# A two-layer graph network: weight rows loaded over two queues, an earlier norm, and layer 1's products split into y and v columns

## Chip, cores and metric

One NeuronCore of a Trainium2 chip runs the whole program. The metric is the device time of one execution in microseconds; the number for the kernel before is the median of three runs.

## What is computed

There are 128 graphs (B) of 128 nodes (N) with 512 features (D), all in float32. Every graph passes through two layers, each behind a layer norm with ReLU, and each adding its result to x. Cut to what matters:

```python
# layer 0
h = maximum(layernorm(x), 0)
Xw = h @ Wv + bv
e = leaky_relu((Xw @ aw[:d])[:, None, :] + (Xw @ aw[d:])[:, :, None] + ab, 0.2)
T = adj * exp(e);  T = T / (T.sum(-1) + 1e-12)
x = x + relu(h @ Wk[0] + bk[0] + (T @ h) @ Wk[1] + bk[1] + (T @ T @ h) @ Wk[2] + bk[2])
# layer 1
h = maximum(layernorm(x), 0)
q, k = split(h @ Wqk);  v = h @ Wv1
w = mask * sum(q * (adj @ (k * mask)), -1) / sqrt(512)
x = x + softmax(w over the nodes)[:, None] * v
```

## The kernel before, in words

The graphs are taken in 64 pairs (`G = 2`, `NP = 64`). Weights are folded first. The columns of Wv times the two halves of aw become two extra columns beside Wk[2] (`r2`, W2). Wk[1] and Wk[0] stand side by side in `r10` (W1). The product of Wq and Wk of layer 1 is formed once (`score_matrix`, L240) as 512 columns, called y's, in `rl[:, :, 0]`; Wv1 is put beside it in `rl[:, :, 1]`. So layer 1 needs only y = h · M and v = h · Wv1, and the score of a node is y times its row of adj · h.

All large products go through `strassen` (L322): the left side is split into two graphs by two halves of the 512 inner features, the right side into two inner halves by two column halves, and seven block products (numbers 1 to 7) stand in for eight. The sums that this needs are formed by VectorE: `left_sums` (L310) per pair, `combine` (L160) once per weight set, four instructions each. Four PSUM banks a, b, c, e collect the blocks; ScalarE copies hand partial results from bank to bank between products (L340 to L348).

Per pair p, the main loop (L625 and on) has TensorE do: `y10(p)` (h · Wk[1] and h · Wk[0] in banks a1, b1, c1, e1), `inner` and `outer` (the two products with T), `y2(p + 1)` for the next pair in banks a2, b2, c2, e2, then `layer1(p - 1)` in the same four banks. `attention` (L390) forms T on VectorE and ScalarE. `norm0` and `norm2` make h; `by_blocks` (L285) sends h to DRAM on SP's queue (`hd`) and reads it back in blocks (`hv`), so that VectorE can transpose it in 32x32 blocks (L299). The first pair and layer 1 of the last pair are transposed on TensorE instead.

In layer 1 before the change, the two column halves of the Strassen split each hold half of y and half of v: block (j, nh) is, for graph j, y[:, half nh] and v[:, half nh]. A score therefore needs both blocks of its graph. For the last pair, `layer1` forms the adj · h products early and scores graph 0 at the sixth product and graph 1 in two half scores (L500), the second of them after the seventh product; `finish_graph` (L529) spreads a score over the partitions by a transpose on TensorE and forms the softmax factor (`weights`, L556), and `result` (L574) adds factor times v to x1 and stores it.

The order on each engine is made by a scheduler from program order and data dependences; `issue_after` and `behind` (L70) add edges that keep an instruction behind a named one on the same engine. Every engine works its instructions off in order. A tile pool's buffers and at most eight outstanding DMAs per kind of queue hold a DMA issue back until an earlier one has landed.

The start is as follows. SP's queue issues x of pair 0 (L121), Wqk in eight pieces (L122 to L125), Wv (`rows(wv0_sb, ...)`, L150), Wk[2] (L151), x of pair 1 (L152) and Wk[1], Wk[0] (L154). `rows` (L144) loads a 512x512 weight in four DMAs, each of which fills 32 partitions (chunk c fills partitions 32c to 32c + 31, from 128 rows of the weight). GpSimd's queue loads small vectors and adj in blocks (`agb`, L93). TensorE runs dummy products (`warm`, L182; four at the start, six more behind the attention vectors, L594), transposes Wqk (`weights_transposed`, L225; ScalarE copies the banks out), transposes h of pair 0, forms the score matrix, then `y2(0)` and `y10(0)`. VectorE forms the attention columns (L199), the sums for r2, then those for r10 (L609) and then attention(0) and pair 1's norm (L618).

Of the kernel before, what the change touches and what calls it, by code (L numbers as in the profile page):

```python
# [15 lines left out]
def kernel(  # L16
# [64 lines left out]
    def load_x(p):  # L81
        xg[p] = loads.tile([P, G, D], FP, name="xg")
        nc.sync.dma_start(xg[p], x[p * G:(p + 1) * G].rearrange("b n d -> n b d"))
# [38 lines left out]
    for c in range(DC):  # L122
        for a in range(2):
            at = slice(a * D, (a + 1) * D)
            nc.sync.dma_start(wqk_sb[:, c, at], wqk[c * P:(c + 1) * P, at])  # L125
# [16 lines left out]
    nc.gpsimd.memset(bias_e[:, 0], 0.0)  # L142

    def rows(dst, w):  # L144

        for c in range(DC):
            nc.sync.dma_start(dst[c * S32:(c + 1) * S32],
                              w[c * P:(c + 1) * P].rearrange("(f a) o -> a f o", a=S32))

    rows(wv0_sb, wv0)  # L150
    rows(r2[:, :, 1:1 + D], wk[2])  # L151
    load_x(1)  # L152
    for k in range(2):
        rows(r10[:, :, k], wk[1 - k])  # L154

    def spread(dst, col):

        nc.tensor.transpose(dst, col.to_broadcast([P, P]), ident)
# [66 lines left out]
    def weights_transposed():  # L225

        banks = [a2, e2, a1, b1, c1, e1]
        for c in range(DC):
            for a in range(2):
                bank = banks[(c * 2 + a) % len(banks)]  # L230
                pt = bank.rearrange("p (o i) -> p o i", o=DC)
                for o in range(DC):
                    at = a * D + o * P
                    nc.tensor.transpose(pt[:, o, :], wqk_sb[:, c, at:at + P], ident)
                if a:
                    nc.scalar.copy(wkt[:, :, c * P:(c + 1) * P], pt)
                else:
                    nc.scalar.copy(wqt[:, :, :, c, :], pt.rearrange("p o (f a) -> p o f a", f=Q))
# [41 lines left out]
    wcols = [const.tile([P, S32], FP, name=f"wcol{i}") for i in range(3)]  # L280
    for t in wcols:
        nc.gpsimd.memset(t, 0.0)
# [190 lines left out]
    def layer1(p, steps={}):  # L473

        if p + 1 < NP:
            yv = late["p"].tile([P, G, 2, 2, HD], FP, name="yv")
        else:
            yv = t10[:, :2].rearrange("p t c o -> p (t c o)").rearrange(
                "p (j h k d) -> p j h k d", j=G, h=2, k=2)
        o = {(j, nh): yv[:, j, nh].rearrange("p k d -> p (k d)") for j in range(G) for nh in range(2)}  # L480
        s = late["p"].tile([P, 2, D], FP, name="s1")
        w = wcols[p % 3]
        last = p == NP - 1

        def end12(b, t):
            nc.vector.tensor_add(o[0, 1], b, t)
            if last:
                score(p, yv, w, a1, 0)
                late["w"] = finish_graph(p, yv, w, 0, b1)
            else:  # L490
                aggregate(p, 0, a2)

        def end22(e, t):
            nc.vector.tensor_add(o[1, 1], e, t)
            if last:
                half_score(e1[:, HD:], yv[:, 1, 1, 0, :], 3)

        def half_score(y, agg, at):
            junk = front.tile([P, D], FP, name="junk", bufs=1)
            nc.vector.scalar_tensor_tensor(junk[:, :HD], y, wscale[:, B - 1:B], agg, op0=OP.mult,  # L500
                                           op1=OP.mult, accum_out=w[:, at:at + 1])

        def end21(c):
            if last:
                half_score(c[:, :HD], agg, 1)
                nc.vector.tensor_add(w[:, 1:2], w[:, 1:2], w[:, 3:4])
            nc.scalar.copy(o[1, 0], c)
            if last:
                factors = finish_graph(p, yv, w, 1, c1)
                behind("peak", result, p, yv, late["w"], slice(0, 1))  # L510
                result(p, yv, factors, slice(1, 2))

        if last:
            agg = front.tile([P, G, 2, HD], FP, name="zz", bufs=1)[:, 0, 0]
            steps = {1: lambda: (aggregate(p, 0, a1), aggregate(p, 1, e1),
                                 nc.scalar.copy(agg, e1[:, :HD]), end(small.tile([P, G], FP, name="peak")))}

        strassen(set2, LEFT2.pop(p), rightl, s, True, {
            (0, 0): lambda a: nc.scalar.copy(o[0, 0], a),
            (1, 1): end22,  # L520
            (0, 1): end12,
            (1, 0): end21}, steps)
        if not last:
            aggregate(p, 1, e2)
            score(p, yv, w, a2, 0)
            score(p, yv, w, e2, 1)
        return yv, w, s

    def finish_graph(p, yv, w, j, bank):  # L529

        pw = bank[:, :G * N].rearrange("p (g n) -> p g n", g=G)
        spread(pw[:, j, :], w[:, j:j + 1])
        return weights(small.tile([P, G], FP, name="peak"), w, pw, slice(j, j + 1))

    def score(p, yv, w, agg, j):

        junk = front.tile([P, D], FP, name="junk", bufs=1)
        b = p * G + j
        nc.vector.scalar_tensor_tensor(
            junk.rearrange("p (k d) -> p k d", k=2), agg.rearrange("p (k d) -> p k d", k=2),  # L540
            wscale[:, b:b + 1], yv[:, j, :, 0, :], op0=OP.mult, op1=OP.mult,
            accum_out=w[:, j:j + 1])
# [31 lines left out]
    def result(p, yv, factors, graphs=slice(0, G)):  # L574
        x1 = X1[p]
        for at, j in enumerate(range(G)[graphs]):
            o = x1[:, j, :].rearrange("p (k d) -> p k d", k=2)
            nc.vector.scalar_tensor_tensor(o, yv[:, j, :, 1, :], factors[:, at:at + 1], o,
                                           op0=OP.mult, op1=OP.add)
        nc.sync.dma_start(out[p * G:(p + 1) * G][graphs].rearrange("b n d -> n b d"), x1[:, graphs])  # L580
# [13 lines left out]
    behind("vector", warm, 6)  # L594
    with tc.issue_after(done["warm"]):
        weights_transposed()
# [7 lines left out]
    with tc.issue_after(done["u"]):  # L604
        right2 = combine(halves(r2, W2), [t2[:, i] for i in range(4)])
    for f in range(Q):
        score_matrix(f)
    with tc.issue_after(done["right"]):
        right10 = combine(halves(r10, HD), pairs(t10))  # L609
    with tc.issue_after(done["right"]), tc.issue_after(done["m"]):  # L610
# [3 lines left out]
        for p in range(2):  # L614
            load_adj(p)
        spread_columns(0)
        attention(0, front.tile([P, D], FP, name="junk", bufs=1)[:, :G * N])
        norm0(1)  # L618
# [6 lines left out]
    for p in range(NP + 1):  # L625
# [38 lines left out]
        if p > 0:  # L664
            def last_left():
# [4 lines left out]
            yv, w, s = layer1(p - 1, {2: lambda: behind("u2", norm2), 3: last_left if p == NP - 1 else lambda: None}  # L670
                              if p < NP else {})
            if p < NP:
                ends.append((p - 1, yv, w, spread_scores(w)))
# [4 lines left out]
        if p == 0:  # L678
            rightl = behind("t", combine, halves(rl, HD), pairs(tl))
# [27 lines left out]
```

## Time and profile before

| What | Value |
|---|---|
| three runs, median | 2324.96 us (2322.57 to 2326.97) |
| profiled execution, its time | 2326.3 us |
| profiled execution, span from first to last instruction | 2324.5 us |
| granted TensorE clock, mean | 0.999 |
| one pair in the middle, 1000 to 1036 us | TensorE busy 36.00 of 36.00 us, VectorE 21.46, ScalarE 16.31, GpSimd 5.33 |
| first score product / y2(0) / y10(0) on TensorE | from 18.27 / 32.11 / 40.95 us |
| layer 1 of the last pair on TensorE | from 2302.22 us |
| last result on VectorE | 2320.29 to 2321.04 us |

In the profile PE is TensorE's matmul, PEld its weight load, DVE is VectorE, ACT is ScalarE, POOL is GpSimd, SP the engine that issues most DMAs; SPq is its queue. L12 is line 12 of the kernel. A float32 product appears as two records, so a 128-row, 512-column product takes about 0.86 us in two passes. A group line has the engine, the line, the operation, the tile written and the tiles read, a count and, in brackets, the idle time before it with what ended it. "A <- B: 1.7, 1, 1.7" in a list of waits says that A stood idle until B, 1.7 us in all, once, at longest 1.7 us. Releasers are inferred from semaphores.

### The profile page before, as it was taken

How to read it: one execution, taken by the hardware profiler on the slowest of the kernel's cores; microseconds unless marked ns; L12 is line 12 of the kernel's file. 1: busy time of each engine (PE TensorE's matmuls, PEld its weight loads, DVE VectorE, ACT ScalarE, POOL GpSimd, SP SyncE). 2: the span in 40 equal slices, each digit the busy share in tenths (PEclk: the TensorE clock that was granted, in tenths of full speed). 3: DMA queues.
4: the chain of work that ended last, by engine and by line, in shares of the span. 5: the costliest groups of instructions: out<-in, count | busy, mean ns of one | idle time of the engine just before them, and what ended most of it. 6: DMA issues, size and time to landing. Idle time of an engine off the chain costs nothing.

```text
span 2324.5 us, 23775 instructions
## 1 busy us (share of the span) xinstructions
PE 2307.6 (99%) x6901; PEld 1292.3 (56%) x6901; DVE 1362.3 (59%) x4134; ACT 1029.2 (44%) x2518; POOL 336.6 (14%) x585
## 2 busy tenths in 40 slices
PE   9999999999999999999999999999999999999998
PEld 5555555555555555555555555555555555555554
DVE  4655656556566566565565665665665656656654
ACT  4444444444444444444444444444444444444443
POOL 2011111111111111111111111111111111111100
PEclk9999999999999999999999999999999999999999
DMA  7533333333333333333333333333333333333311
GB/s 158 138 105 101 110 104 97 115 96 99 114 95 109 106 101 109 104 98 114 98 97 116 93 109 109 100 108 103 98 114 98 97 118 91 109 111 98 105 62 50
DMA packets 248133, 241.56 MB, mean 104 GB/s; under 512 B 25870, under 2 KB 171278, under 8 KB 248002
## 3 DMA queue, kind: packets, MB, share of 16 engines
q1 hardware_dynamic: 227632, 215.01, 29.5%
q0 software_dynamic: 20368, 25.03, 5.0%
q8 instruction: 54, 0.88, 0.2%
q14 instruction: 77, 0.63, 0.1%
q10 hardware_dynamic: 2, 0.00, 0.0%
HBM read 140.20 MB, written 99.74 MB: 103 GB/s over the span
## 4 chain that ended last, share of the span: by engine, by line
PE 96%; DMA 2%; DVE 1%; ACT 0%; issue 0%; SPq 0%; POOL 0%; DVEq 0%; ACTq 0%; POOLq 0%
PE c L333 23%; PE b L333 23%; PE a L333 23%; PE e L333 12%; PE e L471 2%; PE a L471 2%; PE b L459 1%; PE a L449 1%; PE c L449 1%; PE c L459 1%; PE a L459 1%; PE b L449 1%; PE e L459 1%; PE e L449 1%; PE a L420 1%; DMA r<-in_L_gnn_Wk_dram 1%
## 5 line engine op out<-in xcount | busy, mean ns | idle before, releaser
L333 PE MATMUL a<-r,x 128*128 128x257 f32 (+1 forms) x1024 | 373.3, 486 | 4.7 <-DMA ag<-in_adj_dram 1.7
L93 POOL DMA_DIRECT2D agb<-in_adj_dram x256 | 152.2, 599 | 834.0 <-DVE t L406 777.3
L371 DVE TENSOR_TENSOR y<-e,s 128x257 f32<-128x257 f32 x64 | 27.3, 427 | 406.6 <-ACT s L348 406.6
L333 PEld LDWEIGHTS a<-r,x 128*128 128x128 f32 x1024 | 189.1, 190 | 110.7 <-issue 93.2
L333 PE MATMUL a<-rl,x 128*128 128x512 f32 x512 | 240.7, 592 | 0.3 <-PE c L333 0.3
L348 ACT COPY s<-c 128x512 f32<-128x512 f32 (+1 forms) x192 | 97.9, 510 | 209.3 <-PE c L333 209.3
L333 PE MATMUL c<-t,sx 128*128 128x257 f32 (+1 forms) x512 | 186.5, 486 | 1.2 <-ACT c L344 1.2
L333 PE MATMUL b<-t,sx 128*128 128x257 f32 (+1 forms) x512 | 186.5, 487 | 0.2 <-ACT b L340 0.2
L333 PE MATMUL b<-r,sx 128*128 128x257 f32 (+1 forms) x512 | 186.5, 486 | 0.0
L333 PE MATMUL e<-t,sx 128*128 128x257 f32 (+1 forms) x512 | 186.4, 486 | 0.0
L333 PE MATMUL c<-t,x 128*128 128x257 f32 (+1 forms) x512 | 186.4, 486 | 0.0
L379 POOL DMA_DIRECT2D pzd<-pzt x62 | 36.9, 595 | 961.5 <-DVE pzt L377 916.1
L344 ACT COPY c<-b 128x512 f32<-128x512 f32 (+1 forms) x192 | 95.8, 499 | 179.1 <-PE b L333 177.6
L342 ACT COPY s<-e 128x512 f32<-128x512 f32 (+1 forms) x192 | 99.0, 515 | 157.8 <-PE e L333 157.8
L299 DVE STREAM_TRANSPOSE x<-hv 128x512 f32<-128x512 f32 x252 | 163.6, 687 | 8.8 <-DMA hv<-hd 8.7
L333 PEld LDWEIGHTS a<-rl,x 128*128 128x128 f32 x512 | 97.2, 190 | 95.8 <-issue 91.8
L340 ACT COPY b<-a 128x512 f32<-128x512 f32 (+1 forms) x192 | 96.1, 501 | 99.5 <-PE a L333 91.8
L333 PEld LDWEIGHTS c<-t,sx 128*128 128x128 f32 x512 | 96.9, 190 | 70.1 <-issue 60.0
L262 DVE TENSOR_TENSOR r<-r 128x2 f32<-128x2 f32 x128 | 20.0, 156 | 197.1 <-ACT r L261 196.9
L333 PEld LDWEIGHTS b<-t,sx 128*128 128x128 f32 x512 | 97.0, 190 | 69.2 <-issue 46.6
L333 PEld LDWEIGHTS c<-t,x 128*128 128x128 f32 x512 | 96.9, 190 | 69.3 <-issue 60.7
L333 PEld LDWEIGHTS b<-r,sx 128*128 128x128 f32 x512 | 97.1, 190 | 68.2 <-issue 61.2
(214 smaller groups left out, 3919.0 us busy)
## 6 DMA issues: line engine op xcount, KB each, us to landing
hd<-h SPq DMA_DIRECT2D x126, 512.0 KB, 2.8
hv<-hd SPq DMA_DIRECT2D x504, 128.0 KB, 2.6
xg<-in_x_dram SPq DMA_DIRECT2D x64, 512.0 KB, 3.8
out_dram<-x SPq DMA_DIRECT2D x63, 512.0 KB, 4.2
agb<-in_adj_dram POOLq DMA_DIRECT2D x256, 32.0 KB, 2.0
ag<-in_adj_dram SPq DMA_DIRECT2D x64, 128.0 KB, 2.5
pw<-pwd POOLq DMA_DIRECT2D x63, 128.0 KB, 3.3
pz<-pzd POOLq DMA_DIRECT2D x62, 128.0 KB, 3.6
```

What stands on the lines that cost most here:

```text
L93: nc.gpsimd.dma_start(agb[p][c * S32:(c + 1) * S32].rearrange("p g q i -> p (g q) i"), v[c])
L299: nc.vector.transpose(dst[:, j].rearrange("p f (n b) -> p f n b", n=Q), hv[:, j].rearrange("p n (f a) -> p f n a", f=Q))
L333: done["product"] = nc.tensor.matmul(bank, left[i][:, k * P:(k + 1) * P], right[i][:, k], start=(start and k == 0), stop=(k == HC - 1), sk ...
L340: nc.scalar.copy(b, a)
L342: nc.scalar.copy(s[:, 0], e)
L344: done["u2"] = nc.scalar.copy(c, b).ins
L348: nc.scalar.copy(s[:, 1], c)
L371: (1, 1): lambda e, t: nc.vector.tensor_add(y[:, 1, 1], e, t),
L379: nc.gpsimd.dma_start(d.rearrange("g q b -> q g b"), t[::S32])
L449: nc.tensor.matmul(bank[:, :HD], TT[p][:, j, :], y[:, j, nh, 1 - nh:W2 - nh], start=False, stop=True, skip_group_check=True)
L459: nc.tensor.matmul(bank[:, HD:], tt[:, j, :], z[:, j, nh], start=False, stop=True, skip_group_check=True)
L471: nc.tensor.matmul(to, AT[p][:, j, :], h2, start=True, stop=True)
```

## The change

It has three parts.

*Start.* Wqk is loaded in four DMAs instead of eight. A one-column copy on GpSimd, the gate, reads a column of Wqk's second quarter; behind it on GpSimd's queue are issued x of pair 1 and the upper two chunks (partitions 64 to 127) of Wv, Wk[2], Wk[1] and Wk[0]. The lower two chunks stay on SP's queue. The six dummy products ahead of the weight transposes go, and the transposes stand directly behind the attention vectors. Two of the four Wkt copies go from ScalarE to VectorE. The adj loads of pairs 0 and 1 are written ahead of the score matrix, and pair 1's norm ahead of the sums for r10, which now stand behind that norm's `rs`. The three `wcol` memsets on GpSimd are written earlier.

*Layer 1.* The column halves of the Strassen split are now y and v: block (j, 0) is y of graph j, block (j, 1) is v of graph j. The sums for `rl` are taken accordingly, and `score` and `result` read whole contiguous rows of 512.

*Last pair.* `last_layer1` replaces the special cases in `layer1`. Its products run in the order 1, 6, 2, 7, 4, 5, 3. Product 2 completes y of graph 0, product 4 y of graph 1, product 5 v of graph 1 (with v's copy from bank c), and product 3 the rest of v of graph 0, which is added to x1 as factor times bank e and then factor times bank b. The spreads of the two scores stand between the halves of products 4 and 5. Graph 0 is stored in two halves on two queues (ScalarE's and SP's).

```diff
-    def load_x(p):
+    def load_x(p, queue=nc.sync):
         xg[p] = loads.tile([P, G, D], FP, name="xg")
-        nc.sync.dma_start(xg[p], x[p * G:(p + 1) * G].rearrange("b n d -> n b d"))
+        queue.dma_start(xg[p], x[p * G:(p + 1) * G].rearrange("b n d -> n b d"))
...
     for c in range(DC):
-        for a in range(2):
-            at = slice(a * D, (a + 1) * D)
-            nc.sync.dma_start(wqk_sb[:, c, at], wqk[c * P:(c + 1) * P, at])
+        nc.sync.dma_start(wqk_sb[:, c], wqk[c * P:(c + 1) * P])
...
-    def rows(dst, w):
+    def rows(dst, w, chunks=range(DC), queue=nc.sync):
 
-        for c in range(DC):
-            nc.sync.dma_start(dst[c * S32:(c + 1) * S32],
+        for c in chunks:
+            queue.dma_start(dst[c * S32:(c + 1) * S32],
                               w[c * P:(c + 1) * P].rearrange("(f a) o -> a f o", a=S32))
 
-    rows(wv0_sb, wv0)
-    rows(r2[:, :, 1:1 + D], wk[2])
-    load_x(1)
-    for k in range(2):
-        rows(r10[:, :, k], wk[1 - k])
+
+    gate = setup.tile([P, 1], FP, name="gate")
+    done["gate"] = nc.gpsimd.tensor_copy(gate, wqk_sb[:, 1, :1]).ins
+    weights0 = [(wv0_sb, wv0), (r2[:, :, 1:1 + D], wk[2])] + [(r10[:, :, k], wk[1 - k]) for k in range(2)]
+    with tc.issue_after(done["gate"]):
+        load_x(1, nc.gpsimd)
+        for dst, w in weights0:
+            rows(dst, w, range(HC, DC), nc.gpsimd)
+    for dst, w in weights0:
+        rows(dst, w, range(HC))
...
-                    nc.scalar.copy(wkt[:, :, c * P:(c + 1) * P], pt)
+                    (nc.vector.tensor_copy if c < HC else nc.scalar.copy)(wkt[:, :, c * P:(c + 1) * P], pt)
...
+    def last_layer1(p):
+
+
+        left, w, x1 = LEFT2.pop(p), wcols[p % 3], X1[p]
+        agg = front.tile([P, G, 2, HD], FP, name="zz", bufs=1).rearrange("p g k d -> p g (k d)")
+        v = late["p"].tile([P, 2, D], FP, name="s1")[:, 0]
+        a, b, c, e = set2
...
+        product(a, 1, True)
+        nc.scalar.copy(b, a)
+        behind("product", aggregate, p, 0, a1)
+        nc.scalar.copy(agg[:, 0], a1)
+        product(b, 6)
+        nc.scalar.copy(c, b)
+        product(a, 2)
+        score(p, agg[:, 0], w, a, 0)
+        product(c, 7)
+        done["v"] = nc.scalar.copy(v, c).ins
+        behind("product", aggregate, p, 1, e1)
+        behind("v", end, small.tile([P, G], FP, name="peak"))
+        nc.scalar.copy(agg[:, 1], e1)
+        product(c, 4, False, lambda: part.update(pw=spread_score(0, b1)))
+        f0 = factors(0, part["pw"])
+        score(p, agg[:, 1], w, c, 1)
+        product(e, 5, True, lambda: part.update(pw=spread_score(1, c1)))
+        done["v"] = nc.vector.tensor_add(v, e, v).ins
+        product(b, 3)
+        f1 = factors(1, part["pw"])
+        with tc.issue_after(done["v"]):
+            nc.vector.scalar_tensor_tensor(x1[:, 0, :], e, f0, x1[:, 0, :], op0=OP.mult, op1=OP.add)
+        done["x1"] = nc.vector.scalar_tensor_tensor(x1[:, 1, :], v, f1, x1[:, 1, :], op0=OP.mult,
+                                                    op1=OP.add).ins
+        nc.sync.dma_start(out[p * G + 1], x1[:, 1, :])
+        with tc.issue_after(done["x1"]):
+            for i, queue in enumerate((nc.scalar, nc.sync)):
+                at = slice(i * HD, (i + 1) * HD)
+                nc.vector.scalar_tensor_tensor(x1[:, 0, at], b[:, at], f0, x1[:, 0, at], op0=OP.mult,
+                                               op1=OP.add)
+                queue.dma_start(out[p * G, :, at], x1[:, 0, at])
...
-    behind("vector", warm, 6)
-    with tc.issue_after(done["warm"]):
+    with tc.issue_after(done["vector"]):
         weights_transposed()
...
+    for p in range(2):
+        load_adj(p)
     for f in range(Q):
         score_matrix(f)
     with tc.issue_after(done["right"]):
+        norm0(1)
+    with tc.issue_after(done["rs"]):
         right10 = combine(halves(r10, HD), pairs(t10))
     with tc.issue_after(done["right"]), tc.issue_after(done["m"]):
         y2(0)
         seed_a()
         seed_e()
-        for p in range(2):
-            load_adj(p)
         spread_columns(0)
         attention(0, front.tile([P, D], FP, name="junk", bufs=1)[:, :G * N])
-        norm0(1)
...
-            rightl = behind("t", combine, halves(rl, HD), pairs(tl))
+            rightl = behind("t", combine, {(kh, k): rl[:, kh * HC:(kh + 1) * HC, k] for kh in range(2)
+                                            for k in range(2)}, [tl[:, i] for i in range(4)])
```

## The prediction, made before the result was known

> **What bounds the kernel now.** I read the page's busy table first, then a table of TensorE's busy time by stage, then the waits of TensorE in the stages that were not full, then the DMA rate in short slices, and last the end in order of time.
>
> ```profile
> PE 2307.6 (99%) x6901; PEld 1292.3 (56%) x6901; DVE 1362.3 (59%) x4134; ACT 1029.2 (44%) x2518; POOL 336.6 (14%) x585
> ```
>
> TensorE (PE) is the bound; everything else has room. So only time in which PE stands still, or works on something that the change removes, can be won. The stage table (microseconds, length, PE busy and instructions, then the other engines, granted clock, DMA share, GB/s) says where that is:
>
> ```profile
> 9.50:18.27 8.77, 7.52 (x49) 6.38 (x48) 1.00 (x3) 6.23 (x13) 1.74 (x3) 1.00 1.07 214
> 18.27:32.10 13.83, 13.83 (x33) 6.18 (x33) 9.90 (x25) 2.72 (x5) 0.00 (x0) 1.00 1.07 182
> 39.30:84.20 44.90, 38.72 (x114) 20.07 (x115) 30.77 (x82) 18.23 (x44) 6.90 (x12) 1.00 0.58 137
> 84.20:2302.20 2218.00, 2217.45 (x6621) 1242.64 (x6620) 1308.72 (x3982) 989.71 (x2425) 318.97 (x546) 1.00 0.33 102
> 2302.20:2317.10 14.90, 14.18 (x33) 5.81 (x31) 5.84 (x15) 4.08 (x11) 1.67 (x3) 1.00 0.14 44
> 2317.10:2324.50 7.40, 0.62 (x2) 0.27 (x2) 3.31 (x13) 1.53 (x7) 0.00 (x0) 0.67 0.19 72
> ```
>
> From 84 to 2302 us PE is idle for 0.55 us in all: nothing is to be won there. What is loose: the front up to 18.27 us (the first score product's start), 6.2 us of gaps between 39.3 and 84.2, and the 7.4 us after the last product. PE's waits in 33 to 42 us (first line), 42 to 60 (second) and 60 to 75 name the gaps:
>
> ```profile
> PE a L333 <- DMA ag<-in_adj_dram: 1.7, 1, 1.7
> ...
> PE c L333 <- ACT c L344: 1.0, 1, 1.0
> ...
> PE a L333 <- DVE x L299: 1.6, 1, 1.6
> PE a L333 <- ACT a L426: 1.4, 1, 1.4
> ```
>
> The releaser "ag" is an inference; y10(0) reads r10, whose loads land at the same time, and I take those. DMA in short slices:
>
> ```profile
> 7.50:10.00 2.50, 2.50 (x14) 2.50 (x14) 1.00 (x9) 1.45 (x4) 1.23 (x3) 1.00 0.83 313
> 20.00:22.50 2.50, 2.50 (x7) 1.14 (x6) 1.13 (x4) 0.49 (x1) 0.00 (x0) 1.00 1.06 215
> 32.50:35.00 2.50, 2.50 (x12) 1.96 (x12) 0.00 (x0) 1.63 (x4) 0.00 (x0) 1.00 1.06 212
> ```
>
> Loads over all 128 partitions (x, Wqk) run at 313 GB/s; once only weight rows, 32 partitions to a DMA, are left, the rate is 143 to 215 with the engines full.
>
> **The change part by part.** Sums are made against the profiled execution: 2326.3 us with a span of 2324.5. The median of the three runs is 2324.96, 1.3 lower; I take the difference off the median.
>
> *Front.* Wqk's last piece releases PE's last weight transposes at 15.28 us, and the score product starts 3.0 us later:
>
> ```profile
> 12.08 0.64 PE L234 MATMUL b<-ident,tl 128*128 128x128 f32 x4
> ...
> 15.28 0.63 PE L234 MATMUL e<-ident,tl 128*128 128x128 f32 x4 [1.25 <-DMA tl<-in_L_gnn_Wqk_dram]
> ```
>
> x of pair 0 and Wqk are 2.6 MB; by the slices 2.3 MB of all traffic had moved at 10 us, so at 313 GB/s with nothing beside it Wqk would be in at 11. The last piece is late because Wv rows share the engines. In the new kernel the POOL queue starts behind the gate (Wqk's second quarter, about 8 us; GpSimd's copy of one column is not in the trace, by its nearest row, the 128x1 memset, 0.1 us, at most the 0.32 of its mask instruction; then 0.6 us per issue), so x of pair 1 and upper rows compete from about 10 on. I take 13.5 us for the last quarter (11.5 to 15.3), so a start at 16.5: gain 1.8 (0 to 3.5). Behind the gate on POOL stand x of pair 1, eight row loads (9 x 0.6 = 5.4 us of issue) and the eight agb loads of pairs 0 and 1, which move from 5 us to after 16; these are read by the transposes at 46 us, so that is free. SP loses 4 Wqk issues, 8 row loads and one x load; its issues of pair 1's h move up behind its row loads, which are out by about 20 us. The two Wkt copies given to VectorE cost 0.69 us each, beside an idle VectorE (1.00 us busy in 8.77): nothing; on ScalarE the same copies took 0.59.
>
> The six warm products that go (6.80 to 9.7 us) stood before transposes that are now free to start at Wqk's first quarter, about 6.9. Here the rule matters. Transposes cost 0.21 us each up to 12.08 and 0.11 after it. The Trainium skill ("TensorE: Matmul & The Clock Gate", Part 1 and Part 4) says that the array's clock doubles after about 3.4 us of activity and that transposes don't count as such. By the trace the clock held from 12.1 to 18.3 through nearly nothing but transposes, so I take it that they count: they run from 6.9 on and the clock rises at about 12 again. By the rule, the clock stays low until the score product: 2.5 us more between 13.5 and the product's start, and up to 1.7 (half of 3.4) inside it.
>
> *Rows on two queues.* y10(0) could start at 39.29 (the spread's end) but starts at 40.95: 1.66 us for r10. The skill speaks against a gain: "DMA: Bandwidth & Descriptors", Rules for kernel authors, has transfers to disjoint partition halves serialize, and "SBUF — State Buffer" measured only 6% from two. But it also caps 32 or 64 partitions at half of the ports (about 218 GB/s), and the slices show just that: 205 to 215 against 313. Two rings that hold lower and upper halves at once can mix them. At 250 GB/s (an estimate between the two rows) the 7.3 MB of x, Wqk, Wv, Wk land at about 31 us; by the rule, at the old rate less the 0.26 MB of agb put off, at 39.7. y10(0) now could start at 16.5 + 21.0 (18.27 to 39.29) = 37.5, so with 31 us all 1.66 goes; by the rule it starts at 39.7, and front and this step give 1.25 together, not 3.46.
>
> *Pair 1's norm first.* VectorE ran the four sums of r10 (4 x 1.22 us) from 40.93 to 45.7, then attention(0) and the norm mixed, and h went out at 52.8, came back at 59.9. PE waited 1.6 for it; x of pair 2 was issued behind it (57.65, landed 63.6), VectorE's statistics stood waiting for it in front of outer(0), and PE lost 1.4 (row of a, L426). The 1.0 at 48 us is ScalarE's copies behind attention's, late for the same sums. Now the norm (about 3 us) and then the sums (4.9) run while y2(0) and the score product hold PE to 37.5; VectorE stood idle there for 11 us, from 29.9 to 40.9. Behind the norm's wait for x stand the sums and y2(0)'s adds; x of pair 1 is POOL's first load, landed by about 15. I take 3.5 of the 4.0 named us (2.0 to 4.0), and nothing for the other 0.5.
>
> *Layer 1 by columns.* Same instruction counts and sizes: products of 128x512, sums of 128x1024, scores of 128x512 now over contiguous columns (0.75 us before, 0.69 for the contiguous form at L199). PE's 0.43 us per pass is the same for one run of 512 (score product, 3.43 per 8) and two of 256 (r10). Nearest users on PE of this work are 2.6 us off (the e sum at 2268.45, its bank's aggregate at 2271.06). Zero, bounds -0.5 to +0.5 us.
>
> *Last pair.* Before, after the last product:
>
> ```profile
> 2315.21 1.88 PE L333 MATMUL c<-tl,x 128*128 128x512 f32 x4
> 2317.13 0.48 DVE L500 SCALAR_TENSOR_TENSOR junk<-c,wscale,zz 128x256 f32<-128x256 f32 x1
> 2320.29 0.75 DVE L578 SCALAR_TENSOR_TENSOR x<-t,wcol,x 128x512 f32<-128x512 f32 x1
> ```
>
> The score, its spread, maximum, exponential and result follow the product: 4.1 us to 2321.04, then 3.46 for the store. After: PE has seven products (1.72), two aggregates (0.86), two spreads (0.11): 14.0 from 2302.2, plus an estimated 0.5 for a wait of the second spread, whose score stands behind pair 62's results on VectorE: 2316.7. (Pair 62's exponentials, which held product 7 by 0.7 us, now stand behind the v copy.) Both factors are then ready or nearly. VectorE has left: v's sum (0.69, from 2315.5), two results (0.75 each) and two halves (0.43 each): 2318.5; store 3.1 to 3.4 (half the size; half stores took 2.2 to land). End at 2321.7: gain 2.8 (1.5 to 3.8).
>
> Sum: 1.8 + 1.7 + 3.5 + 2.8 = 9.8; 2325.0 - 9.8 = 2315.2 us.
>
> **The rivals.**
> 1. *Cold clock*, by the skill's rule above: 4.2 us back, 2319.4. For it: the warm products go. Against: the held clock in 12 to 18 us.
> 2. *Queues serialize*: 2.2 back, 2317.4. For it: the skill's rule; against it: the 215 beside 313 GB/s, which looks like half of the ports.
> 3. *Slower: GpSimd's queue is late.* r10's upper half and x of pair 1 hang on 2.6 MB from that queue. Norm and last pair give 6.3; the case decides against us if r10 lands more than 6.3 us after 40.95, at 47.2, that is below 70 GB/s from 10 us on; at 55 GB/s it lands at 57.6, +10.3 us: 2335. Against: in the page's queue table this queue moved 25.03 MB in 5.0% of the span, 216 GB/s while busy.
> 4. *More than thought*: Wqk in at 11.5, all named gaps and 3.8 at the end: 3.5 + 1.7 + 4.0 + 3.8 = 13.0, 2312.0.
> 5. *Little happens*: rivals 1 and 2 at once with VectorE's chain filling the end (gain 1.5): about 2 to 5 us, 2321.5.
>
> **How the numbers follow.** Forecast 0.58 (2312.5 to 2318), rivals 1 and 2 together 0.22, rival 4 0.10, rival 5 0.07, rival 3 0.03. A measurement of this kernel can tell about 0.2% from no change, that is 4.65 us: below 2320.3 lie the forecast, rival 4 and nearly all of 1 and 2: 0.88; same 0.09 (rival 5 and the rest); slower 0.03. The range 2310.5 to 2320 holds the forecast, rival 4 and most of 1 and 2.
>
> **What would show it.** Right: score product's start near 16.5 us; slices from 12 to 30 us near 250 GB/s; y10(0) at about 37.5 with no wait; no waits on L299 and L426 in 50 to 70 us; PE idle after 40 us at about 1 us; the stage from pair 2 on full as before; under 5.5 us from the last product to the end. Wrong: transposes of 0.21 us after 13 us (rival 1); 200 GB/s in 12 to 35 us (rival 2); an xg or r load from POOL landing after 40 us (rival 3); gaps in PE in the middle of the run, or a last product that waits over 1 us for a spread.

## The result, and the profile after

The changed kernel's median is 2314.56 us (four executions, 2313.56 to 2318.47) beside 2325.12 us for the kernel before: ratio 0.9958, 95% interval 0.9941 to 0.9976. Nine later executions gave a median of 2318.17 us (2313.78 to 2320.26) beside 2326.26: ratio 0.9964, 0.9953 to 0.9975. So the change takes off 8 to 11 us. The last experiment shows where one of the longer executions lost its time.

The profiled execution took 2314.45 us with a span of 2312.7, that is 11.8 less than the span before. The busy table of the page:

```profile
PE 2303.2 (100%) x6889; PEld 1291.1 (56%) x6889; DVE 1362.6 (59%) x4134; ACT 1026.8 (44%) x2514; POOL 341.9 (15%) x595
```

TensorE's busy time was 2307.6 us before, so by this table it is only 4.4 us shorter; the other 7.4 us of the gain were idle time. The stage table (start and end, length, then busy time and instructions of PE, PEld, DVE, ACT and POOL, granted clock, DMA share, GB/s):

```profile
32.10:39.30 7.20, 4.71 (x21) 3.84 (x21) 6.19 (x10) 3.88 (x9) 0.00 (x0) 1.00 0.33 114
39.30:84.20 44.90, 44.56 (x147) 26.91 (x148) 26.44 (x76) 19.00 (x47) 7.19 (x13) 1.00 0.49 117
84.20:2300.00 2215.80, 2215.80 (x6605) 1239.61 (x6604) 1306.10 (x3977) 988.68 (x2422) 320.39 (x549) 1.00 0.35 102
```

From 39.3 to 84.2 us TensorE was busy for 38.72 us before and is now for 44.56 us: the stalls are gone. The first row shows a new hole instead: 2.5 us idle inside y2(0). TensorE in order of time (start, duration, engine, line, operation, tile, count, idle time before it):

```profile
12.58 0.63 PE L240 MATMUL a<-ident,tl 128*128 128x128 f32 x4 [0.40 <-DMA tl<-in_L_gnn_Wqk_dram]
...
16.01 3.70 PE L250 MATMUL a<-wkt,wqt 128*128 128x512 f32 x8
...
34.47 1.14 PE L336 MATMUL b<-t,sx 128*128 128x257 f32 x4 [2.72 <-ACT b L343]
...
39.96 1.96 PE L336 MATMUL a<-r,x 128*128 128x512 f32 x4
...
2305.56 0.32 PE L164 MATMUL c<-ident,wcol 128*128 128x128 f32 x1 [0.61 <-DVE junk L560]
...
2306.58 1.88 PE L506 MATMUL b<-rl,sx 128*128 128x512 f32 x4
```

The score product starts at 16.01 instead of 18.27; product 6 of y2(0) waits 2.72 us for ScalarE; y10(0) starts at 39.96 without a wait for r10; the second spread of the last pair waits 0.61, and the last product starts at 2306.58. ScalarE around that new wait:

```profile
32.63 1.52 ACT L279 ACTIVATE h<-xg,rs 128x512 f32<-128x512 f32 x2 [0.54 <-DVE rs L273]
34.06 0.36 ACT L343 COPY b<-a 128x257 f32<-128x257 f32 x1
```

The copy that TensorE needs stands behind the two h instructions of pair 1's norm, and these waited for VectorE's `rs`. Two of the DMA slices:

```profile
20.00:22.50 2.50, 2.50 (x7) 1.12 (x6) 1.21 (x3) 0.93 (x2) 1.18 (x2) 1.00 1.05 297
22.50:25.00 2.50, 2.50 (x7) 1.14 (x6) 2.36 (x9) 0.59 (x1) 1.16 (x2) 1.00 1.06 292
```

The mean of the five slices from 15 to 27.5 us is 282 GB/s, 190 before; the loads end at about 31.5 us, 39.5 before.

Two landmarks of TensorE, y10(0) and y10(2): the first line and the second are of the kernel before, the third is of the changed kernel (its y10(0) stands above).

```profile
40.95 1.96 PE L333 MATMUL a<-r,x 128*128 128x512 f32 x4 [1.66 <-DMA ag<-in_adj_dram]
...
106.33 1.88 PE L333 MATMUL a<-r,x 128*128 128x512 f32 x4
```

```profile
97.98 1.88 PE L336 MATMUL a<-r,x 128*128 128x512 f32 x4
```

All landmarks in the two profiled executions, and what each stretch gave:

| Landmark (start, us) | before | after | gained in the stretch that ends there |
|---|---|---|---|
| first score product | 18.27 | 16.01 | 2.26 |
| y10(0) | 40.95 | 39.96 | -1.27 (1.66 for r10 won, 2.72 lost to ScalarE, 0.21 elsewhere) |
| y10(2) | 106.33 | 97.98 | 7.36 |
| last pair's layer 1 | 2302.22 | 2293.37 | 0.50 |
| end of the span | 2324.5 | 2312.7 | 2.95 |

The sum is 11.8. Each figure compares one execution with one, and the landing times of the loads differ between executions, so the first two rows are the least sure: in two more profiles of the changed kernel (below) the score product starts at 17.32 and 16.33 us.

### The profile page after: what moved, and what is told of

The parts are those of the page before. It is cut to its first block, busy times and chain, and to the rows that moved or that the text cites. A ratio compares the mean times of both kernels' runs of the same rounds, so it can differ in the third digit from the quotient of the medians.

```text
span 2312.7 us, 23740 instructions
## 1 busy us (share of the span) xinstructions
PE 2303.2 (100%) x6889; PEld 1291.1 (56%) x6889; DVE 1362.6 (59%) x4134; ACT 1026.8 (44%) x2514; POOL 341.9 (15%) x595
## 4 chain that ended last, share of the span: by engine, by line
PE 98%; DMA 1%; DVE 1%; issue 0%; ACT 0%; POOL 0%; DVEq 0%; SPq 0%
PE b L336 24%; PE c L336 24%; PE a L336 24%; PE e L336 12%; PE a L474 2%; PE e L474 2%; PE a L452 1%; PE b L452 1%; PE b L462 1%; PE e L462 1%; PE c L452 1%; PE c L462 1%; PE e L452 1%; PE a L462 1%; PE a L423 1%; DMA t<-in_L_gnn_Wv_dram 1%
## 5 line engine op out<-in xcount | busy, mean ns | idle before, releaser
L302 DVE STREAM_TRANSPOSE x<-hv 128x512 f32<-128x512 f32 x252 | 163.5, 686 | 1.9 <-DMA hv<-hd 1.7
L336 PEld LDWEIGHTS e<-t,sx 128*128 128x128 f32 x512 | 96.9, 189 | 68.4 <-issue 60.7
```

The costliest lines, as they stand in the source:

```text
L302: nc.vector.transpose(dst[:, j].rearrange("p f (n b) -> p f n b", n=Q), hv[:, j].rearrange("p n (f a) -> p f n a", f=Q))
L336: done["product"] = nc.tensor.matmul(bank, left[i][:, k * P:(k + 1) * P], right[i][:, k], start=(start and k == 0), stop=(k == HC - 1), sk ...
```

## The experiments

Theory A is the prediction's: two queues that fill separate halves of the partitions raise the rate, the earlier norm removes the stalls of the first pairs, the last pair's order shortens the end, and the columns are worth nothing. Theory B in each text is the rival for that step. The diffs are cut (`...` marks what is left out) and are against the changed kernel unless the text says otherwise.

**The start alone.** Layer 1 and the last pair are those of before.

```diff
-            if p == NP:
-                last_layer1(p - 1)
-                break
...
-            rightl = behind("t", combine, {(kh, k): rl[:, kh * HC:(kh + 1) * HC, k] for kh in range(2)
-                                            for k in range(2)}, [tl[:, i] for i in range(4)])
+            rightl = behind("t", combine, halves(rl, HD), pairs(tl))
```

> The new start with the old layer 1 and the old last pair. Theory A (start and last pair are two separate gains, the columns give nothing): y10(2) starts at 98.0 us as in the changed kernel (106.5 before), the last pair's layer 1 at 2293.4, the stage from there to the end stays 22.3 us as before, span 2315.6. Rival (the y and v columns also shorten the middle): last pair's layer 1 later than 2293.4 by more than 0.5 us.

Measured: 2317.28 us (six executions), ratio 0.9971 (0.9959 to 0.9983). y10(2) starts at 97.92 us and the last pair at 2293.30, both as in the changed kernel to 0.1 us; from there to the end it takes 22.0 us (22.3 before). The start gives its whole share by itself. The stretch from y10(2) to the last pair takes 2195.4 us here, with the old columns, as in the changed kernel (2195.4), and not 2195.9 as before.

**Layer 1 and the last pair alone.** The same edit the other way, on the kernel before.

```diff
+            if p == NP:
+                last_layer1(p - 1)
+                break
...
-            rightl = behind("t", combine, halves(rl, HD), pairs(tl))
+            rightl = behind("t", combine, {(kh, k): rl[:, kh * HC:(kh + 1) * HC, k] for kh in range(2)
+                                            for k in range(2)}, [tl[:, i] for i in range(4)])
```

> The old start with the new layer 1 and the new last pair. Theory A: y10(2) at 106.5 us as before, last pair's layer 1 at 2302.2, 19.3 us from there to the end, span 2321.5. Rival: columns shorten the middle, last pair's layer 1 before 2301.7.

Measured: 2322.98 us (12 executions), ratio 0.9993 (0.9983 to 1.0003): by the times alone not told from nothing. The trace says more. From y10(2), at 105.34 us, to the last pair it took 2195.9 us, with the new columns, just as before (2195.9): the columns give nothing, and the 0.5 us that this stretch gained comes with the new start. From the last pair's start to the last product's start there are 13.21 us in both this and the changed kernel, and the end is 20.1 us after that start instead of the 19.3 expected; of the 0.8 us, 0.6 lie in the two last stores, which took 2.6 us to land here and 2.0 in the changed kernel. Over all the profiles with the new last pair this end took 19.3 us in nine and 19.8 to 20.1 us in three, against 22.0 and 22.3 with the old last pair: its gain is 1.9 to 3.0 us.

**All weight rows on one queue.**

```diff
-    gate = setup.tile([P, 1], FP, name="gate")
-    done["gate"] = nc.gpsimd.tensor_copy(gate, wqk_sb[:, 1, :1]).ins
...
+    rows(wv0_sb, wv0)
+    rows(r2[:, :, 1:1 + D], wk[2])
+    load_x(1)
+    for k in range(2):
+        rows(r10[:, :, k], wk[1 - k])
```

> The changed kernel with all weight rows and x of pair 1 on SP's queue again and no gate. Theory A (the two queues matter through VectorE: r10 lands at about 39.5 us, its four sums, and y2(0)'s adds and attention(0) behind them, come 6 us later): the product y10(0) starts near 40 but PE stalls inside it and before y2(1), y10(2) starts at about 102, 4 us later than 98.0. Rival B (what holds y10(0) at 40.0 us is ScalarE's copy behind the norm, so the queues are worth nothing): y10(2) at 98.0 to 98.5.

Measured: 2325.24 us (12 executions), ratio 0.9997 (0.9985 to 1.0009): by the median nothing of the gain is left without the second queue. The profiled execution, at 2322.89 us one of the shorter ones, keeps 3.4 us of the 11.8, of which 2.2 are the last pair's. Two slices, and the worst of the stalls that came back:

```profile
15.00:17.50 2.50, 2.50 (x14) 2.50 (x14) 0.16 (x1) 1.34 (x3) 0.00 (x0) 0.50 1.08 207
...
22.50:25.00 2.50, 2.50 (x7) 1.14 (x6) 2.39 (x8) 1.18 (x2) 0.00 (x0) 1.00 1.09 163
```

```profile
50.38 0.53 PE L419 MATMUL a<-ident,t 128*128 128x128 f32 x2 [1.89 <-DVE t L405]
```

and, earlier in the same run, TensorE's transposes:

```profile
14.36 1.04 PE L236 MATMUL a<-ident,tl 128*128 128x128 f32 x4 [2.11 <-DMA tl<-in_L_gnn_Wqk_dram]
15.20 1.06 PE L236 MATMUL e<-ident,tl 128*128 128x128 f32 x4
...
17.86 0.60 PE L306 MATMUL e<-ident,h 128*128 128x128 f32 x4
```

The rate from 15 to 27.5 us is 188 GB/s, the sums for r10 start at 41.18 us (33.22 in the changed kernel) and y10(2) at 105.31: 7.3 us later, where theory A expected 4. From y10(0) to y10(2) it takes 64.11 us, 58.02 in the changed kernel: the norm alone, ahead of sums that still wait for late rows, brings little. The first row also shows a granted clock of 0.50, behind 2.11 us in which the transposes waited for Wqk. At 17.86 us the transposes are fast again, after 3.5 us in which TensorE ran transposes and four products of one column and nothing else.

**The norm back behind attention.**

```diff
     with tc.issue_after(done["right"]):
-        norm0(1)
-    with tc.issue_after(done["rs"]):
         right10 = combine(halves(r10, HD), pairs(t10))
...
         attention(0, front.tile([P, D], FP, name="junk", bufs=1)[:, :G * N])
+        norm0(1)
```

> The changed kernel with pair 1's norm behind attention(0) again, sums of r10 directly behind those of r2. Both theories: the 2.7 us wait for ScalarE's copy in y2(0) goes and y10(0) starts near 37.3. Theory A (the norm's place is worth more than the named waits, about 4 to 6 us counted from start to start): y2(1) waits for h from DRAM, y10(2) starts at 100 to 102, 2 to 4 us later than 98.0. Rival B (worth the named 3 to 3.5 us, nearly all given back by the new wait): y10(2) at 97 to 98.7.

Measured: 2324.79 us (12 executions), ratio 1.0000 (0.9992 to 1.0009). TensorE:

```profile
13.19 1.09 PE L240 MATMUL a<-ident,tl 128*128 128x128 f32 x4 [1.62 <-DMA tl<-in_L_gnn_Wqk_dram]
...
19.73 5.46 PE L250 MATMUL a<-wkt,wqt 128*128 128x512 f32 x8
...
63.45 2.08 PE L336 MATMUL a<-r,x 128*128 128x257 f32 x4 [4.80 <-DVE x L302]
```

The wait for ScalarE in y2(0) is gone, but TensorE waits 4.80 us for the transposed h of pair 1 (L302), and the clock is half behind it. y10(2) starts at 108.34 us, where theory A expected 100 to 102. From y10(0) to y10(2) it takes 65.74 us, 58.02 in the changed kernel: the norm's place is worth 7.7 us there (some 2 of them the half clock). y10(0) itself missed its expectation (42.60 us, not 37.3) for another reason: the transposes waited 1.62 us for Wqk, the clock fell, and the first score product took 5.46 us instead of 3.70.

**Two queues, both into the same halves.** Both queues take one chunk of each half in the same order, so that two queues are kept and only the split by halves goes.

```diff
-            rows(dst, w, range(HC, DC), nc.gpsimd)
-    for dst, w in weights0:
-        rows(dst, w, range(HC))
+        for c in (1, 3):
+            for dst, w in weights0:
+                rows(dst, w, (c,), nc.gpsimd)
+    for c in (0, 2):
+        for dst, w in weights0:
+            rows(dst, w, (c,))
```

> The changed kernel with the chunks dealt out so that both queues write the same half of the partitions at the same time: SP's queue loads chunk 0 of all four weights, then chunk 2; GpSimd's queue chunk 1 of all, then chunk 3. Queues, sizes and counts are the same. Theory A (the halves have separate ports and only a mix of both fills them): the DMA rate from 15 to 27 us falls from 270 to 297 GB/s to 200 to 220, loads end near 38 us instead of 31.5. Rival B (two queues simply keep more in flight): 270 to 300 GB/s as before, loads end near 31.5.

Measured in one execution: 2329.47 us.

```profile
22.50:25.00 2.50, 2.50 (x4) 1.01 (x3) 0.91 (x3) 0.00 (x0) 0.58 (x1) 0.51 1.02 208
```

With both queues in one half the slices from 17.5 to 27.5 us run at 208 to 223 GB/s, and the loads end at about 37 us. So a second queue alone does not bring 282 GB/s; both halves have to be loaded at once. (One queue that takes its chunks from the two halves in turn was not tried.) The time itself says little of the rate, since the order of the weights changes too: Wv lands only at 29.8 us, and behind the 2.94 us wait for Wqk the clock is at half until 25 us.

**The six dummy products back.**

```diff
-    with tc.issue_after(done["vector"]):
+    behind("vector", warm, 6)
+    with tc.issue_after(done["warm"]):
         weights_transposed()
```

> The changed kernel with the six dummy products ahead of the weight transposes again. Theory A (transposes count as activity, and behind the front VectorE's chain from Wv's landing sets y10(0)): transposes start near 9.5, the clock rises near 12, the score product starts about 1.3 us later than 16.0, and y10(0) still starts at 40.0, y10(2) at 98.0. Rival B (PE's front is the bound): y10(0) and y10(2) 1.3 us later. Rival C (the clock rises earlier with real products ahead of it): transposes of 0.11 us before 11 us.

Measured in one execution: 2314.06 us, y10(2) at 97.59 us (97.98 without them). Their removal was worth nothing that shows: they stand in time in which TensorE waits for Wqk anyway (1.68 us here). Rival C's sign came, transposes only 0.11 us apart from 10.05 us on, but the dummy products don't explain it. Over all profiles the first fast group of transposes starts between 10.05 and 12.08 us in the five with dummy products ahead, between 10.48 and 14.23 us in the nine without: the time of the rise scatters.

**ScalarE's first copy of y2(0) ahead of pair 1's norm.**

```diff
-        nc.scalar.copy(b, a)
+        done["u1"] = nc.scalar.copy(b, a).ins
...
-    with tc.issue_after(done["right"]):
-        norm0(1)
-    with tc.issue_after(done["rs"]):
-        right10 = combine(halves(r10, HD), pairs(t10))
+    def norm1():
+        with tc.issue_after(done["u1"]):
+            norm0(1)
+        with tc.issue_after(done["rs"]):
+            late["r10"] = combine(halves(r10, HD), pairs(t10))
...
-        y2(0)
+        y2(0, {5: norm1})
```

The adds of y2 on VectorE are put behind the sums for r10 as well (not shown).

> The changed kernel with ScalarE's first bank copy of y2(0) ordered ahead of pair 1's norm, and y2's adds on VectorE behind the sums of r10. Theory A (the wait of 2.7 us is only the order on ScalarE): y10(0) starts at 37.3 and y10(2) at 95.4, span 2310.1. Rival B (the sums of r10 or attention(0) are late next): y10(2) at 97.5 to 98, span over 2312.

Measured: 2313.61 us (four executions, 2313.10 to 2314.19), ratio 0.9943 (0.9926 to 0.9959). ScalarE, then TensorE:

```profile
31.73 0.34 ACT L343 COPY b<-a 128x257 f32<-128x257 f32 x1
...
33.56 1.52 ACT L279 ACTIVATE h<-xg,rs 128x512 f32<-128x512 f32 x2
```

```profile
81.03 1.96 PE L336 MATMUL a<-rl,x 128*128 128x512 f32 x4 [0.62 <-DVE x L302]
```

The 2.72 us wait is gone and y10(0) starts at 37.69 us, where the prediction had put it. At y10(2) 1.3 of the 2.3 us are left (96.69 beside 97.98): h of pair 1 is now formed 0.9 us later, and a wait of 0.62 us for a transpose on VectorE (L302) has come up ahead of layer 1 of pair 0. That the later h causes this wait was not followed.

**Wv ahead of x of pair 1 on GpSimd's queue.**

```diff
-        load_x(1, nc.gpsimd)
-        for dst, w in weights0:
+        for i, (dst, w) in enumerate(weights0):
             rows(dst, w, range(HC, DC), nc.gpsimd)
+            if i == 0:
+                load_x(1, nc.gpsimd)
```

> The changed kernel with Wv's upper rows ahead of pair 1's x on GpSimd's queue. Theory A (VectorE's chain from Wv's landing at 21.2 us sets the norm, and so the copy behind it): Wv lands near 17.5, sums of r2 end near 26.5, h is done before the copy is wanted, y10(0) at 37.5, y10(2) at 95.6, span 2310.3. Rival B (Wk[2] or x of pair 1 lands too late to follow): VectorE's chain moves by under 1 us, y10(2) at 97 to 98.

Measured: 2318.8 us (five executions, 2313.07 to 2320.45), ratio 0.9959 (0.9944 to 0.9975). Wv is no longer waited for (its columns start at 19.61 us), and the wait for ScalarE shrinks to 0.63 us. But the transposes wait 2.09 us for Wqk's last piece, the clock is 0.78 and 0.54 in 12.5 to 17.5 us, the score product starts at 18.74 and y10(2) at 98.65. That the new order delays Wqk is not shown: the piece is let in at 13.66 us here, and at 12.58 and 13.89 in two profiles of the changed kernel. No gain shows in the times either, and they scatter as widely as the changed kernel's.

**The changed kernel again, and two versions beside it.** The first is unaltered. The second has the copy first and the dummy products, the third Wv's rows first as well.

> The changed kernel once more, unaltered, so that the two versions below stand beside it on one chip and so that its front can be compared between two executions. Theory A (how long the weight transposes wait for Wqk's last piece differs from execution to execution, and with it the granted clock and the start of the score product): a median between 2313.5 and 2316, single times spread over about 4 us, and a profile whose score product starts anywhere from 16.0 to 19.7 us, with y10(2) later than 97.98 us only if the clock fell. Theory B (the changed kernel's front is fixed by its order of DMAs): the score product starts within 0.2 us of 16.01 and the times agree within 1 us.

> ScalarE's first copy of y2(0) ahead of pair 1's norm, and the six dummy products put back ahead of the weight transposes. Theory A (the dummy products bring the clock up before the transposes and take nothing that is needed, and the copy takes the 2.72 us wait away): score product from 15.5 to 17.5 us at full clock, y10(2) at 96 to 97 us, 2312.5 to 2314 us, with single times closer together than those of the changed kernel. Theory B (the clock's fall is set by the wait for Wqk's last piece alone, dummy products or not): some executions still 2 to 5 us longer, a spread as wide as the changed kernel's, and a median no better than 2314.5.

> As the version with the copy first and the dummy products, and Wv's upper rows issued ahead of x of pair 1 on GpSimd's queue. Theory A (with the dummy products in front, a later last piece of Wqk no longer costs the clock, so Wv's earlier landing is a clear gain for VectorE's chain): Wv's columns from about 19.6 us, the score product at full clock from 16.5 to 18 us, y10(2) at 95.5 to 97 us, 2312 to 2313.5 us. Theory B (Wv's rows delay Wqk's last piece by as much as they give back, and the clock falls in some executions): score product from 18.7 us, 2314 to 2318 us.

Measured: unaltered 2318.17 us (nine executions, 2313.78 to 2320.26), ratio 0.9964 (0.9953 to 0.9975); copy and dummy products 2313.33 us (five, 2312.69 to 2314.54), 0.9948 (0.9933 to 0.9963); with Wv first 2314.59 us (five, 2313.04 to 2317.32), 0.9953 (0.9939 to 0.9967). In the second of these kernels TensorE waits for nothing over 0.4 us between 30 and 100 us, and y10(2) starts at 96.55. It is the best kernel of this study: the slowest of its five executions beats seven of the changed kernel's nine, though the intervals overlap. In the third the dummy products did not save the clock. TensorE's transposes, then a slice:

```profile
16.44 0.69 PE L241 MATMUL a<-ident,tl 128*128 128x128 f32 x4 [1.14 <-DMA tl<-in_L_gnn_Wqk_dram]
16.93 1.06 PE L241 MATMUL e<-ident,tl 128*128 128x128 f32 x4
```

```profile
17.50:20.00 2.50, 2.50 (x14) 2.50 (x13) 0.16 (x1) 1.17 (x4) 0.00 (x0) 0.50 1.07 235
```

Waits of 2.31 and 1.14 us for Wqk, then half the clock; the score product starts at 21.52 us and y10(2) at 100.77. The unaltered kernel's median missed what both theories expected, and its times spread over 6.5 us. Its profile was of a short execution (2313.78 us): the score product later, at 17.32, but Wv earlier, at 20.50, so that ScalarE's wait was 0.69 us and y10(2) came at 97.32. Theory A was right that the start differs between executions, but the start of the score product doesn't set the time by itself. Where ScalarE's copy b is waited for, Wv's landing sets it: in four profiles (the first, the start alone, this one and the long one below) product 6 of y2(0) starts 13.21 to 13.24 us after VectorE's first column of Wv, while the score product starts anywhere from 16.01 to 17.66 us.

**The changed kernel in one of its long executions.** Unaltered.

> The changed kernel, unaltered, profiled a third time, since its single times scatter from 2313.6 to 2320.3 us and both profiles so far were of short executions. If the time is below 2315.5, the stages stand as in the two profiles: y10(2) between 97.3 and 98.0 us. If it is above 2317, theory A (the clock falls while the transposes wait for Wqk's last piece) has a granted clock below 0.8 in one slice between 12 and 20 us, the score product from 18.5 us or later and y10(2) at 100 us or later, all else unchanged; theory B (late weight rows or a late x of pair 1) has a full clock, a wait for ScalarE's copy b of over 4 us or a wait for r10, and y10(2) at 100 us or later; theory C (something else, later) has y10(2) at 97 to 98.5 us and the loss behind it.

Measured: 2319.93 us. VectorE's first column of Wv, TensorE, and a slice:

```profile
23.70 0.69 DVE L205 SCALAR_TENSOR_TENSOR junk<-t,aw_bc 128x512 f32<-128x512 f32 x1 [5.64 <-DMA t<-in_L_gnn_Wv_dram]
```

```profile
36.91 2.08 PE L336 MATMUL b<-t,sx 128*128 128x257 f32 x4 [4.85 <-ACT b L343]
38.78 1.92 PE L336 MATMUL a<-r,x 128*128 128x257 f32 x4
```

```profile
37.50:40.00 2.50, 2.50 (x7) 2.01 (x6) 2.47 (x3) 0.50 (x2) 0.00 (x0) 0.50 0.56 209
```

The front is as in the first profile (score product at 16.33 us). But Wv lands at 23.70 us instead of 21.25 and 20.50, the wait for ScalarE's copy b is 4.85 us instead of 2.72 and 0.69, and behind it the clock is half for some 6 us: the products of 128x257 take 1.92 us for four records, not 1.03. From product 6 to the end of y2(0) (36.91 to 44.39) it takes 7.5 us, 4.4 in the profile before this one. y10(2) starts at 103.47 us, 5.5 after the first profile's; its time is 5.5 longer. Of these, 2.45 us are Wv's later landing and 3.0 the slow products. Theory B holds, but for the full clock that it expected. The two kernels with the copy first and x of pair 1 still ahead don't have this wait in their profiles, and their nine executions scatter by 1.9 us, while the 14 of the changed kernel scatter by 6.7. Why Wv landed later here the trace doesn't say; x of pair 1, ahead of its upper rows on GpSimd's queue, landed later too (at about 21.2 us, 19.0 in the first profile). That Wv's landing makes every long execution is not shown: the others left no trace, and two, of 2319.68 and 2319.79 us, list a mean granted clock of 1.000 where this one has 0.998, so they lost their time without such a fall.

## Why the prediction came out as it did

The median was 0.6 us under the forecast of 2315.2; that of the nine later executions was 3.0 over it. The mechanism was right in the main. That the number fits so closely is partly luck: a loss of 2.7 us that the prediction did not see at y10(0) stands against a gain of pair 1's norm that it booked 3.9 us too low, and the median itself moves by 3.6 us between the two groups of executions.

- *Front, 1.8 us foretold, 2.26 found.* Wqk's last piece was let in at 12.58 us, not 13.5 (13.89 in another execution, which leaves 0.95 us of gain). Transposes ran from 6.80 us, and they were fast from 12.58 us on as it had been said, so transposes count towards the clock; by the Trainium skill's rule that they don't ("TensorE: Matmul & The Clock Gate", Part 4) the group at 12.58 us should have taken 1.06 us, as the ones before it, not 0.63. That the products before 6.80 us alone brought the rise is unlikely: in the run with one queue the clock came back behind nothing but transposes and four products of one column. But rival 1 had a true core that the prediction had not placed: where the transposes wait long for Wqk, the clock falls and the score product starts at 18.7 to 21.7 us.
- *Rows on two queues, 1.66 us foretold at y10(0).* That wait is gone and r10's loads ended at 31.5 us (31 foretold). The rate was 282 GB/s, not 250. The rule of "DMA: Bandwidth & Descriptors" (Rules for kernel authors) that disjoint halves serialize doesn't hold here, with many row loads in flight on each queue, and 282 over 190 is far more than the 6% of "SBUF — State Buffer" ("Can I just issue two DMAs to hit both halves?"); with both queues in the same half it was 208 to 223. The prediction took 205 to 215 for the rate of one half; the slices of 143 to 175 GB/s in between, which it names, it left unexplained, and they stay so. The worth of the step was booked too narrowly: without it 7.3 us are missing at y10(2), since the norm's step lives on early rows. From y10(0) to y10(2) the norm's place without the second queue saved only 1.3 us and the second queue without the norm's place some 1.7 (the half clock taken out), both together 7.4.
- *Pair 1's norm first, 3.5 us foretold, 7.4 found: this term was mis-sized.* No wait is left on the transposes (L302 now) or the aggregate's row. The term was taken from the list of waits, 4.0 us; all idle time in that stretch was 4.85. In TensorE's rows the last matmul of a run lasts 0.59 us though the next may start 0.43 after it, so each gap hides up to 0.16 us. Counted from start to start, y10(0) to y10(2) took 65.38 us for about 57.5 us of passes (an estimate from 0.43 us for 512 columns and 0.22 for 256): 7.9 us were loose, and 0.5 are now.
- *y10(0) at 37.5 us without a wait: this step failed.* It came at 39.96. The prediction let the norm run on VectorE's idle time, and did not count the norm's two h instructions on ScalarE, which stand ahead of the copies that y2(0) needs and wait for `rs`; that comes behind the sums for r2, and these behind Wv's landing. (x of pair 1, for which 15 us was taken, landed at about 19.0, still ahead of Wv, and was not waited for.) The copy put first removes the 2.72 us and brings y10(0) to 37.69, so this is shown.
- *Columns, nothing foretold:* 2195.9 us from y10(2) to the last pair with the old start, 2195.4 with the new, whichever the columns. Right.
- *Last pair, 2.8 us foretold, 2.95 found* (1.9 to 3.0 over all profiles). The last product ends 14.93 us after the start (14.5 foretold), the wait for the second spread was 0.61 us (0.5 foretold), and from that product to the end it is 4.4 us (5.0 foretold). Right.

So the sum on record, 1.8 + 1.7 + 3.5 + 2.8 = 9.8, was 2.26 + 1.66 - 2.72 - 0.21 + 7.36 + 0.50 + 2.95 = 11.8 in the profile (10.6 between the medians). Rival 3 never came near: GpSimd's first x load was issued at 7.88 us and seven of its eight row loads by 12.45. The eighth had to wait until one of the eight loads in flight, that of x, had landed:

```profile
18.98 0.55 POOL L148 DMA_DIRECT2D r<-in_L_gnn_Wk_dram  x1 [6.53 <-DMA xg<-in_x_dram]
```

## What to carry to other kernels

When a step moves ahead of another, walk down every engine that it uses, not only the idle one: the norm was free on VectorE and stood in ScalarE's queue ahead of a copy on the critical path. Measure what stalls are worth from start to start of a stretch against its passes, not by the sum of idle times. Loads that fill 32 partitions each went a half faster here (282 GB/s, not 190) from two queues with one half of the partitions each; when each of them landed set the pace of the engine that reads them. Neither this nor the earlier norm was worth much alone.

## What the runs showed that was not expected

- The granted clock falls behind some short waits of TensorE, and not from a fixed length on. At the weight transposes it held through waits of 1.24 to 1.47 us, 1.68 and 1.86 (the last two with dummy products ahead), and fell after 1.62, 2.09, 2.11, 2.94 and after 2.31 with 1.14. Later in the run it held through 1.89 us and through the 2.72 us of the first profile, and fell after 4.32, 4.80 and 4.85. Such a fall is dear: the 4.85 us were followed by 3.0 us lost in slow products, and behind the 1.62 us it took 6.54 us from that transpose to the score product instead of 3.43, and 5.29 instead of 3.54 for its first bank.
- The clock's row says 1.00 in the first 10 to 12 us, in which transposes take 0.21 us each, twice what they take later. The slow first stage is to be read from durations.
- The landing time of one load among many in flight differs between executions of one program: in three executions of the changed kernel the first column of Wv starts at 20.50, 21.25 and 23.70 us, and in two of them Wqk's last piece is let in at 12.58 and 13.89. In the last of them 2.45 us of later landing made 5.5 us of time, for the clock fell behind the longer wait.
